# A projection between two large products, in seven half-size products for two row blocks at a time

## The chip, the core and the metric

The kernel runs on one core of a Trainium2 chip. Its engines work side by side, each through its own queue in order: TensorE (PE in the profile; its weight loads are PEld), VectorE (DVE), ScalarE (ACT), GpSimd (POOL) and SyncE (SP), which only issues transfers. Transfers (DMA) are issued from SP's and from POOL's queue. The metric is device time in microseconds, the median of the runs.

## What is computed

Two graph layers on 4096 nodes with 512 features, all in float32. `adj` is 4096 x 4096 and sparse, `W` is 512 x 512.

```python
# layer 0
mask = adj > 0
head = mask / max(sqrt(sum(mask * mask, axis=-1)), EPS)
inc  = adj + head
x = layernorm(x + (inc @ x) / sum(inc, axis=-1))
# layer 1
A2 = adj + eye
dscale = diagonal(A2) ** -0.5
temp = A2 @ x @ W.T
x = layernorm(x + relu((dscale[:, None] * A2 * dscale[None, :]) @ temp))
```

So there are three products with a 4096 x 4096 matrix, and between the second and the third stands the projection by `W.T`, which this change touches.

## The kernel before

All three large products are done by Strassen's scheme in Winograd's form, in which a product of 2 x 2 blocks takes seven block products instead of eight, with sums of blocks before and after. Layer 0 uses one level of it. The products of layer 1 use two: the code numbers them k = 2 (`A2 @ x`) and k = 3 (`A2` times the projected and scaled features).

**Steps of k = 2 and k = 3.** The list `steps` runs over k, over two column halves s, over the seven outer products p in the order of `ORDER[k]`, and over eight blocks kk of the summed dimension. One step (n) is seven matmuls of the inner level, `multiply2`, line 271: 128 x 128 weights are a block of features, the moving operand is 128 x 512 of the adjacency matrix or of sums of its blocks. Each of the seven collects in a PSUM bank of its own (q0 to q6) over the eight kk. The eighth bank, q7, is `spare()`. A float32 matmul shows as two instructions in the profile.

**What VectorE does for a step.** `prepare(n + 2)` (line 226) makes the sums of the adjacency blocks for two steps ahead (`add_up`, lines 166, 168 and 169) in one of three buffers; `sum_b` (lines 255 to 257) makes those of the feature blocks for every second step. In some outer products of k = 2, `prepare` also adds a block of the matrix to a resident one ("raise"), at line 234 before or at line 242 after the sums.

**After eight kk** `outer(k, p, acc)` (line 697) decodes: `inner` (line 676) reads the seven banks and makes four quarters out of them, by two ACT copies into `p1` and `p5` and seven VectorE operations with `u2` and `u3`; each quarter is put straight into a quarter tile of C (`into`) or goes by way of a tile `y` and from there into one or two quarter tiles (`by_way`). For k = 2, p = 7 it goes by way and updates both c21 (line 720) and c22 (line 695) for each of the four parts. Updates of whole quarter tiles, 128 x 2048, are put on the list `deferred`; the loop pops one per step.

**Projection.** C is kept transposed: features on the partitions, nodes along the free dimension. `DONE` says after which p a half of the features' rows is complete: the upper index half h = 1 after p = 7 and h = 0 after p = 3, for each s. Then eight row blocks of 128 nodes go into `queue`, and the loop takes one up per step with 1 <= kk <= 5. `project` (line 748) does four matmuls (line 755) with 512 columns of `wt` into the spare bank; ACT scales the result by `dscale` into a tile z (line 758). For h = 1 the two halves of z are written to DRAM as the operands B21 and B22 of k = 3 (line 760). For h = 0, B11 is written (line 764), B21 and B22 of the same rows are read back (line 763), and one step later `outer_sums` (lines 127 to 133) makes T1 to T4 on VectorE in a tile t, which goes to DRAM (line 769). All these transfers are in POOL's queue. SP loads the operands in `load_b` (line 248), in the order of k = 3: B21, B22, T1, B11, T2, T3, T4.

**Layer 0** shares tiles with it: `combine` (line 494) decodes into two z tiles of four, `layer0` normalises them in place, `operands` (line 533) sends them and their sums t to DRAM.

**The end.** In the last outer product `layer1_first` (line 807) turns back, rectifies and takes statistics of the half of the output features that is already complete. The last three steps are not multiplied in the loop; `finish` (line 826) does their matmuls product by product (line 839), decodes as each comes, turns each of eight row blocks back (`turn`: blocks with r = 0 by two transposes at line 775, blocks with r = 1 by four matmuls that subtract at the same time, lines 863 and 864), rectifies on ACT, adds x on POOL (line 867), takes statistics (`measure`) and normalises and writes out (`leave`), on ACT or VectorE. The order of these calls is written out by hand.

The order of all work is the order of the program text; nothing reorders it. An engine that waits holds up all that stands behind in its queue.

Of the kernel before, what the change touches and what calls it, by code (L numbers as in the profile page):

```python
# [26 lines left out]
def tile_adj_resnorm_d2(  # L27
# [56 lines left out]
    small = ctx.enter_context(tc.tile_pool(name="small", bufs=6))  # L84
# [27 lines left out]
    dscale = const.tile([P, NB], F32, name="dscale")  # L112
    nc.gpsimd.dma_start(out=dscale, in_=diag)
# [80 lines left out]
    queue, later, deferred = [], [], []  # L194
# [31 lines left out]
    def prepare(n):  # L226
# [14 lines left out]
        if k == 2 and p in (1, 2) and kk < EARLY:  # L241
            nc.vector.tensor_add(r, r, a)
# [28 lines left out]
    def multiply2(n, acc, between=None):  # L271
        kk = steps[n][3]
        for m, (right, left) in enumerate(factors(n)):
            if m == 3 and between is not None:
                between()
            nc.tensor.matmul(acc[m], left, right, start=(kk == 0), stop=(kk == NQ - 1))  # L276
# [101 lines left out]
    def spread(j, part):  # L378

        if part == 0:  # L380
            n = small.tile([P, 2], F32, name="n")
# [104 lines left out]
    def take(h, acc):  # L486

        y = row_tile("z", 4)
# [5 lines left out]
    def combine(acc):  # L494

        q1, q2, q6, q5, q7, q3, q4 = acc
        top, low = row_tile("z", 4), row_tile("z", 4)
        p1, p5 = row_tile("p1", 1)[:, 0:W], row_tile("p5", 1)[:, 0:W]
        u2, u3 = row_tile("u2", 1)[:, 0:H], row_tile("u3", 1)[:, 0:H]
        deg = small.tile([P, 2], F32, name="deg")  # L500
# [19 lines left out]
    def layer0(j, C):  # L520

        rd = small.tile([P, 2], F32, name="rd")
# [28 lines left out]
    deg0 = small.tile([P, 2], F32, name="deg")  # L551
# [76 lines left out]
    for n in range(NC, NP * NC):  # L628
# [21 lines left out]
        if j == 1 and c == 1:  # L650
            nc.vector.tensor_scalar(dscale, dscale, 1.0, None, op0=ALU.add)
            nc.scalar.activation(dscale, dscale, AF.Sqrt)
            nc.vector.reciprocal(dscale, dscale)
        if c == 1:
# [15 lines left out]
    wt = accs.tile([P, ND, D], F32, name="wt")  # L670
# [26 lines left out]
    def outer(k, p, acc):  # L697
# [13 lines left out]
        if k == 2:  # L711
# [6 lines left out]
            elif p == 7:  # L718
                def then(i, y):
                    nc.vector.tensor_sub(c21[:, i, :], c21[:, i, :], y)  # L720
                    less(c22[:, i, :], y, c12[:, i, :])
                by_way(then)
# [25 lines left out]
    def project(h, item):  # L748

        j, r, cols = item  # L750
        b = j + h * NP
        pv = spare()
        for f in range(2):
            for e in range(2):
                nc.tensor.matmul(pv, C_of[2][h][f][:, 2 * r + e, cols], wt[:, 2 * f + e, :],  # L755
                                 start=(f + e == 0), stop=(f + e == 2))
        z = row_tile("z", 4)
        nc.scalar.activation(z, pv, AF.Copy, scale=dscale[:, b:b + 1])
        if h:
            nc.gpsimd.dma_start(out=in_outer(3, j, slice(B21, B22 + 1)), in_=split(z))  # L760
            return
        low = split(row_tile("z", 4))
        nc.gpsimd.dma_start(out=low, in_=in_outer(3, j, slice(B21, B22 + 1)))
# [261 lines left out]
```

## Time and profile before

| | before |
|---|---|
| median of the runs | 2298.86 us |
| runs | 2297.68, 2298.86, 3728.19 us |
| profiled execution: time, span | 2299.48 us, 2297.7 us |
| PE busy, share of the span | 2271.1 us, 99% |
| DVE busy | 1797.6 us, 78% |
| ACT busy | 346.8 us, 15% |
| POOL busy | 242.4 us, 11% |
| granted TensorE clock | 0.998 |

"Busy" is time in which an engine executes; the span runs from the first to the last instruction of the profiled execution. "A <- B" in a list of waits means that engine and line A stood idle until B had finished; the numbers are us in total, times, longest. In the order of time each row is the start in us, the duration in us, then engine, line, operation and tiles. The chain that ended last is followed back from the last instruction to what released it.

### The profile page before, as it was taken

Reading aid. Unit: us, or ns where it says so; the run is one execution under the profiler, and the core shown is the slowest. Engines: PE = TensorE matmul, PEld = TensorE weight load, DVE = VectorE, ACT = ScalarE, POOL = GpSimd, SP = SyncE. Lnnn points to the kernel's source line nnn. Section 1 sums busy time; section 2 is a strip of 40 time slices with the busy share of each in tenths; the row PEclk is TensorE's granted clock in tenths of the full one; section 3 lists DMA queues with packets and bytes.
Section 4 is the critical chain, followed back from the end, with each engine's and each line's share of the span. In section 5 each row is a group of like instructions: output and inputs, shape, how many; then the busy total and the mean of one; then the engine's idle time right before and its main releaser. Section 6 shows DMA issues by size and latency. Waiting matters only on the chain.

```text
span 2297.7 us, 20993 instructions
## 1 busy us (share of the span) xinstructions
PE 2271.1 (99%) x7191; PEld 1348.0 (59%) x7191; DVE 1797.6 (78%) x2553; ACT 346.8 (15%) x798; POOL 242.4 (11%) x393
## 2 busy tenths in 40 slices
PE   8999999999999999999999999999999999999997
PEld 6888888888888844444444444444444444444444
DVE  6988898988988787787666778676566788767787
ACT  4333233232231000000000000000000011200013
POOL 0111112211122100000111100010100000100012
PEclk9999999999999999999999999999999999999999
DMA  9788778777876576574566856476665666765672
GB/s 331 268 279 264 261 233 272 273 263 261 249 246 230 203 270 255 190 270 178 231 242 235 296 187 251 158 284 252 236 238 216 226 249 238 256 248 213 225 256 106
DMA packets 149482, 553.64 MB, mean 241 GB/s; under 512 B 16592, under 2 KB 24800, under 8 KB 110976
## 3 DMA queue, kind: packets, MB, share of 16 engines
q1 hardware_dynamic: 114624, 417.38, 51.1%
q0 software_dynamic: 34752, 134.93, 16.5%
q8 instruction: 57, 0.93, 0.2%
q14 instruction: 49, 0.40, 0.1%
HBM read 438.98 MB, written 113.26 MB: 240 GB/s over the span
## 4 chain that ended last, share of the span: by engine, by line
PE 85%; DMA 5%; DVE 4%; issue 4%; ACT 1%; POOL 1%; SPq 0%; ACTq 0%; POOLq 0%; DVEq 0%
PE q L276 55%; PE q L470 25%; PE q L755 5%; DMA nat<-adj 2%; DMA b<-x 1%; DMA a<-adj_r 1%; DVE a L440 1%; DVE mask L433 1%; PE q L775 1%; DVE s L166 1%; ACT nat L330 1%; PE q L839 0%; DVE sr L414 0%; DMA a<-adj_q 0%; DMA oa<-sr 0%
## 5 line engine op out<-in xcount | busy, mean ns | idle before, releaser
L276 PE MATMUL q<-s,ts 128*128 128x512 f32 x1326 | 605.9, 592 | 1.7 <-DVE u L682 1.6
L470 PE MATMUL q<-b,s 128*128 128x256 f32 (+1 forms) x1920 | 454.4, 379 | 0.7 <-DVE s L168 0.7
L276 PEld LDWEIGHTS q<-s,ts 128*128 128x128 f32 x1326 | 251.5, 190 | 318.4 <-issue 289.3
L166 DVE TENSOR_TENSOR s<-a 128x1024 f32<-128x1024 f32 x236 | 288.7, 1223 | 167.7 <-PE q L276 128.9
L470 PEld LDWEIGHTS q<-b,s 128*128 128x128 f32 x1920 | 363.1, 189 | 54.0 <-DVE s L168 1.1
L470 PE MATMUL q<-b,a 128*128 128x258 f32 (+1 forms) x1440 | 352.1, 380 | 1.1 <-ACT p L501 1.1
L276 PE MATMUL q<-a,tr 128*128 128x512 f32 x692 | 325.6, 593 | 1.6 <-DMA a<-adj_r 1.6
L470 PEld LDWEIGHTS q<-b,a 128*128 128x128 f32 x1440 | 272.7, 189 | 40.7 <-ACT p L501 1.5
L276 PE MATMUL q<-s,tr 128*128 128x512 f32 x442 | 225.7, 592 | 0.0
L276 PEld LDWEIGHTS q<-a,tr 128*128 128x128 f32 x692 | 129.3, 190 | 156.0 <-issue 149.2
L330 ACT ACTIVATE nat<-nat,tiny 128x512 f32<-128x512 f32 x240 | 171.3, 717 | 244.0 <-DMA nat<-adj 243.7
L276 PE MATMUL q<-a,ts 128*128 128x512 f32 x346 | 177.0, 593 | 1.2 <-DVE y L687 1.2
L168 DVE TENSOR_TENSOR s<-a,s 128x512 f32<-128x512 f32 x236 | 163.3, 692 | 8.1
L169 DVE TENSOR_TENSOR s<-a,s 128x512 f32<-128x512 f32 x236 | 163.3, 692 | 8.0
L433 DVE SCALAR_TENSOR_TENSOR mask<-a,sc 128x1024 f32<-128x1024 f32 (+2 forms) x129 | 154.1, 1196 | 2.1
L440 DVE TENSOR_TENSOR a<-a,mask 128x1024 f32<-128x1024 f32 x123 | 150.7, 1225 | 6.3
L276 PEld LDWEIGHTS q<-s,tr 128*128 128x128 f32 x442 | 84.0, 190 | 105.7 <-issue 97.6
L680 ACT COPY p<-q 128x512 f32<-128x512 f32 x27 | 15.8, 585 | 730.2 <-PE q L276 730.2
L276 PEld LDWEIGHTS q<-a,ts 128*128 128x128 f32 x346 | 65.5, 190 | 84.9 <-issue 76.1
L755 PE MATMUL q<-wt,c 128*128 128x512 f32 x256 | 115.1, 592 | 0.0
L166 DVE TENSOR_TENSOR s<-r 128x1024 f32<-128x1024 f32 x48 | 58.7, 1223 | 56.2 <-PE q L276 50.8
L276 PE MATMUL q<-r,tr 128*128 128x512 f32 x192 | 90.2, 592 | 0.0
(167 smaller groups left out, 1684.1 us busy)
## 6 DMA issues: line engine op xcount, KB each, us to landing
a<-adj_r SPq DMA_DIRECT2D x112, 1024.0 KB, 6.0
a<-oa SPq DMA_DIRECT2D x80, 1024.0 KB, 5.3
nat<-adj SPq DMA_DIRECT2D x240, 256.0 KB, 7.6
a<-adj_q SPq DMA_DIRECT2D x60, 1024.0 KB, 6.3
tr<-ob SPq DMA_DIRECT2D x112, 512.0 KB, 3.8
oa<-sr POOLq DMA_DIRECT2D x64, 512.0 KB, 7.7
oa<-r POOLq DMA_DIRECT2D x32, 1024.0 KB, 6.1
y<-x POOLq DMA_DIRECT2D x64, 256.0 KB, 6.3
```

The source lines that it names most:

```text
L166: nc.vector.tensor_add(s[:, S3:S1 + 1, :], a[:, A11:A22 + 1, :], a[:, A21, :].unsqueeze(1).to_broadcast([P, 2, w]))
L168: nc.vector.tensor_add(s[:, S2, :], a[:, A11, :], s[:, S1, :])
L169: nc.vector.tensor_add(s[:, S4, :], a[:, A12, :], s[:, S2, :])
L276: nc.tensor.matmul(acc[m], left, right, start=(kk == 0), stop=(kk == NQ - 1))
L330: nc.scalar.activation(y, a, AF.Sign, bias=tiny, scale=2.0 ** 64, accum_out=accum)
L433: nc.vector.scalar_tensor_tensor(m, v, 0.0, s.unsqueeze(1).to_broadcast(list(v.shape)), op0=ALU.is_gt, op1=ALU.mult)
L440: nc.vector.tensor_add(z, z, y)
L470: nc.tensor.matmul(acc[m][:, 0:w], left, b[:, right, 0:w], start=(kk == 0), stop=(kk == NP - 1))
L680: nc.scalar.copy(p1, q1)
L755: nc.tensor.matmul(pv, C_of[2][h][f][:, 2 * r + e, cols], wt[:, 2 * f + e, :], start=(f + e == 0), stop=(f + e == 2))
L775: nc.tensor.transpose(ps[:, at + i * P:at + (i + 1) * P], C_of[3][h][d // 2][:, 2 * r + d % 2, cols], ident)
```

## The change

Two row blocks, r = 0 and r = 1 of the same n, are projected together as a 2 x 2 block product: their C blocks (r by feature half f) times `wt` (feature half f by output half). `wt` holds seven operands, four loaded and T1 to T4 computed once in step 4 (T4 is then taken as one of the seven). The seven products are of two matmuls with 256 columns each into the spare bank, ACT copies each out into one of eight half tiles, and they stand between the matmuls of three successive steps. The four sums of C blocks are made on Pool, the combinations of the products on DVE. The eight blocks of a half become four pairs; two of them are begun per outer product, at kk = 2 and kk = 4.

T2, T3 and T4 of k = 3 are no longer made from a read-back: the half h = 1 writes its share (with a negative scale `nscale` where it is needed), and the half h = 0 adds its own to it in DRAM by accumulating DMAs.

Around it: the decode of p = 7 goes straight into c22, and both updates are deferred; the raises of line 242 are held until after the decode; while pairs are waiting, all deferred updates are done at once. z tiles are two instead of four, some pools of small tiles shrink. In the last outer product the addition of x in `layer1_first` moves from DVE to Pool and ahead by a step. In `finish` the last quarter is decoded, subtracted on DVE and turned back ahead of the remaining statistics, all eight blocks by transposes, and which blocks ACT normalises is set by hand.

```diff
-    small = ctx.enter_context(tc.tile_pool(name="small", bufs=6))
+    small = ctx.enter_context(tc.tile_pool(name="small", bufs=4))
@@ prepare
-            nc.vector.tensor_add(r, r, a)
+            raises.append(lambda: nc.vector.tensor_add(r, r, a))
@@ multiply2
-            if m == 3 and between is not None:
-                between()
+            if m in between:
+                between[m]()
@@ combine
-        top, low = row_tile("z", 4), row_tile("z", 4)
+        top, low = row_tile("z", 2), row_tile("z", 2)
@@ outer, k == 2
             elif p == 7:
-                def then(i, y):
-                    nc.vector.tensor_sub(c21[:, i, :], c21[:, i, :], y)
-                    less(c22[:, i, :], y, c12[:, i, :])
-                by_way(then)
+                into(c22)
+                deferred.extend((lambda: nc.vector.tensor_sub(c21, c21, c22), lambda: less(c22, c22, c12)))
@@ project
-        pv = spare()
-        for f in range(2):
-            for e in range(2):
-                nc.tensor.matmul(pv, C_of[2][h][f][:, 2 * r + e, cols], wt[:, 2 * f + e, :],
-                                 start=(f + e == 0), stop=(f + e == 2))
-        z = row_tile("z", 4)
-        nc.scalar.activation(z, pv, AF.Copy, scale=dscale[:, b:b + 1])
...
+    def project(h, s, n, first):
+        cols = slice(n * P, (n + 1) * P)
+        a11, a12, a21, a22 = (C_of[2][h][f][:, 2 * r:2 * r + 2, cols] for r in range(2) for f in range(2))
+        if first:
+            pools["places"] = [t[:, i * H:(i + 1) * H] for t in (row_tile(t, 1) for t in ("p1", "p5", "u2", "u3")) for i in range(2)]
+        places = [pools["places"][i] for i in (range(7) if first else (7, 1, 0, 6, 3, 2, 4))]
+        q = []
+        def product(left, right):
+            def now():
+                ps = spare()[:, 0:H]
+                for e in range(2):
+                    nc.tensor.matmul(ps, left[:, e, :], wt[:, right, e, :], start=(e == 0), stop=(e == 1))
+                q.append(places[len(q)])
+                nc.scalar.copy(q[-1], ps)
+            return now
+        def sums():
+            s1, s2, s3, s4 = (y[:, 2 * i:2 * i + 2, :] for y in (row_tile("y", 2, (P, 4, P)) for _ in range(2)) for i in range(2))
+            nc.gpsimd.tensor_add(s1, a21, a22)
+            nc.gpsimd.tensor_add(s2, a11, s1)
+            nc.gpsimd.tensor_add(s3, a11, a21)
+            nc.gpsimd.tensor_add(s4, a12, s2)
+            return s1, s2, s3, s4
+        if first:
+            yield {1: product(a11, B11), 3: product(a12, B21), 5: product(a22, T4)}
+            s1, s2, s3, s4 = sums()
+            yield
+            yield {1: product(s2, T2), 3: product(s3, T3), 5: product(s1, T1)}
+            yield
+            yield {1: product(s4, B22)}
+        else:
+            yield {4: product(a11, B11)}
+            s1, s2, s3, s4 = sums()
+            yield
+            yield {1: product(a12, B21), 3: product(a22, T4), 5: product(s2, T2)}
+            yield
+            yield {1: product(s3, T3), 3: product(s1, T1), 5: product(s4, B22)}
+        q1, q2, q4, q6, q7, q5, q3 = q
+        z = [row_tile("z", 2) for _ in range(2)]
+        nc.vector.tensor_add(z[0][:, 0:H], q2, q1)
+        nc.vector.tensor_add(q6, q6, q1)
+        nc.vector.tensor_add(q7, q7, q6)
+        nc.vector.tensor_add(q6, q6, q5)
+        nc.vector.tensor_add(z[0][:, H:D], q3, q6)
+        nc.vector.tensor_sub(z[1][:, 0:H], q4, q7)
+        nc.vector.scalar_tensor_tensor(z[1][:, H:D], q7, -1.0, q5, op0=ALU.mult, op1=ALU.subtract)
+        t = row_tile("t", 1, (P, 4, H))
+        for r in range(2):
+            nc.vector.tensor_sub(t[:, 2 * r, :], z[r][:, 0:H], z[r][:, H:D])
+        for r in range(2):
+            leave_operands(h, r * NQ + s * SB + n, z[r], t[:, 2 * r, :], t[:, 2 * r + 1, :])
+        yield
+    def leave_operands(h, j, z, t, m):
+        b = j + h * NP
+        def scaled(o, y, by=dscale):
+            nc.scalar.activation(o, y, AF.Copy, scale=by[:, b:b + 1])
+        def put(op, y, **how):
+            nc.gpsimd.dma_start(out=in_outer(3, j, slice(op, op + 1)), in_=y.unsqueeze(1), **how)
+        first, second = z[:, 0:H], z[:, H:D]
         if h:
+            scaled(m, second, nscale)
+            scaled(z, z)
+            scaled(t, t)
             nc.gpsimd.dma_start(out=in_outer(3, j, slice(B21, B22 + 1)), in_=split(z))
+            put(T2, m)
+            put(T3, second)
+            put(T4, t)
+        else:
+            scaled(m, t, nscale)
+            scaled(t, t)
+            scaled(first, first)
+            scaled(second, second, nscale)
+            put(B11, first)
+            put(T1, t)
+            put(T2, m, accum_op=ALU.add)
+            put(T3, second, accum_op=ALU.add)
+            put(T4, m, accum_op=ALU.add)
@@ layer1_first
+            nc.gpsimd.tensor_add(o[:, H:D], o[:, H:D], y[:, H:D])
...
-                add(o[:, H:D], y[:, H:D])
@@ finish
-            if i < 2:
-                nc.vector.tensor_sub(c21[:, i, :], y, c21[:, i, :])
-            else:
-                lower[i] = y
+            nc.vector.tensor_sub(c21[:, i, :], y, c21[:, i, :])
...
         measure(0)
         measure(1)
-        leave(0)
+        put(2, lambda o: nc.vector.tensor_sub(o, acc[q4], u3))
+        for t in range(4, 8):
+            turn(t)
         measure(2)
-        leave(1)
-        put(2, lambda o: nc.vector.tensor_sub(o, acc[q4], u3))
-        turn(4)
         measure(3)
-        leave(2)
-        turn(5)
-        leave(3)
+        leave(0, True)
+        leave(1, False)
+        leave(2, True)
         measure(4)
...
@@ the loop
-        if deferred:
+        while deferred:
             deferred.pop(0)()
+            if not pairs:
+                break
+        between = {3: lambda: take_up(items.pop(0))} if len(items) > 1 else {}
+        if kk in (2, 4) and pairs:
+            going.append(project(*pairs.pop(0), kk == 2))
+        for pair in going:
+            between.update(next(pair))
         if n < len(steps) - TAIL:
-            multiply2(n, acc, (lambda: take_up(items.pop(0))) if len(items) > 1 else None)
+            multiply2(n, acc, between)
...
+        elif n == 4:
+            outer_sums(wt[:, T1:T4 + 1], wt[:, B11], wt[:, T4], wt[:, B21], wt[:, B22])
...
+        for pair in going[::-1]:
+            next(pair)
+        if kk in (4, 6):
+            del going[:1]
...
+        while raises:
+            raises.pop(0)()
```

## The prediction

> **What bounds the kernel now.** I read four views in this order: the page's busy table, the chain that ended last, the list of what TensorE (PE) waited for, and the order of time at two places.
>
> ```profile
> PE 2271.1 (99%) x7191; PEld 1348.0 (59%) x7191; DVE 1797.6 (78%) x2553; ACT 346.8 (15%) x798; POOL 242.4 (11%) x393
> PE 85%; DMA 5%; DVE 4%; issue 4%; ACT 1%; POOL 1%; SPq 0%; ACTq 0%; POOLq 0%; DVEq 0%
> ...
> 124.75 533.41 PE q L470 x2460
> ...
> 1061.08 3.43 PE q L755 x8
> 1064.51 6.01 PE q L276 x14
> ```
> PE is busy throughout and 85% of the chain is PE, so a removed matmul is worth its full time if nothing new makes PE wait. The last three rows give prices. One step (14 instructions of 512 columns) is 6.01 us, 0.429 each. The projection of one row block (8 such) is 3.43 us. In layer 0, 2460 instructions of some 256 columns take 533.41 us, 0.217 each: half the columns cost half the time.
>
> ```profile
> PE q L863 <- DVE y L911: 2.9, 1, 2.9
> PE q L276 <- DVE u L682: 1.6, 2, 0.8
> ...
> PE q L276 <- DVE y L687: 1.2, 2, 0.6
> ...
> PE q L839 <- DVE s L168: 0.7, 1, 0.7
> ```
> These are PE's waits outside layer 0's start that the change touches (us in total, times, longest). L682 and L687 are the decode of outer product 7 in the first chain of products, twice; L839 and L863 are the tail.
>
> **Projection: PE.** It goes: 32 blocks of 3.43 us, 109.8 us. It gets 16 pairs of 7 products, each 2 matmuls of 2 instructions with 256 columns: 28 x 0.217 = 6.07 us a pair, 97.1 us. **-12.6 us**, all on the chain. The interleaving costs PE nothing by itself: the transposes (L775) in the last outer product lie between matmuls and the steps around them keep 6.01.
>
> **Decode of product 7.** The order of time at the first of the two places:
>
> ```profile
> 1044.76 2.29 DVE r L242
> 1047.04 0.61 DVE y L681
> 1047.65 0.02 issue
> 1047.68 0.69 DVE c L720
> 1048.37 0.60 DVE c L695
> 1048.97 0.61 DVE u L682
> ```
> Each PSUM read is followed by two updates of C (L720, L695), and ahead of it all VectorE (DVE) does the 2.29 us raise of L242. PE's step begun at 1046.92 takes until 1054.90, 7.98 us instead of 6.01: 1.97 lost; the second place (1440.32 to 1448.45) lost 2.12. The change decodes straight into C, which is one operation per read as for products 4, 5 and 1 (no PE wait there), does the updates (2.29 + 2.28) in the next step, and moves all raises behind the decode. **-4.0 us.** The raises issue no DMA; what they hold longer is the slot of their `a` tile, so SP's next load into it may start later, but PE reads that tile later than the raise. What is late next: DVE now has 2.6 (operand sums) + 1.5 (feature sums) + 4.6 + 2.3 = 11 us in that step of 6.01. Counting on from the decode, the second prepare behind it ends about 18.6 us after the step's start and PE needs it at 20.6: 2 us to spare, because the step ahead of it is longer by three products.
>
> **Projection: DVE, ACT and Pool.** Per pair DVE gets 9 operations of 128x256 at the spacing of L127/L132 (0.34, dependent 0.45): 3.3 us; gone are four per block in one half (64 x about 0.36 = 23 us), added 53: 30 us net over the some 490 us of these stages, in which DVE was busy 323. ACT gets 7 PSUM copies (0.37, L489) and 6 or 8 scalings a pair; a 128x256 one out of SBUF is not in the trace: 0.37 (L779's spacing) to 0.82 (L161, twice the width), I take 0.48 (L161's spacing of 0.70 less 256 columns of L779). Pool gets four adds a pair (L867, 0.72) and 8 or 10 DMA issues, 0.54 to 0.91 each where the rows show them: 8 to 10 us a pair, with a pair every some 16 us. All this is covered if it keeps up, and there are three new waits to check.
> First, PE waits at each product for the ACT copy of the one before (one PSUM bank): two matmuls lie between, 1.72 us, against about 0.6. But ACT is in order, and the first pair's scalings, which wait for DVE, stand ahead of the second pair's copies. Counted from the start of the step in which the first pair ends (7.75 us long: 6.01 and two products): DVE's prepare starts at -0.66 (its buffer is free before the step's last matmul) and takes 2.58, sum_b 1.50, so the combination starts at 3.4, its differences t end at 6.5 and 6.8; ACT is through at 9.5 (upper half) to 10.5 (lower half), the blocked copy at 10.9 at the latest, and PE needs it at 11.2. It holds with 0.3 to 1.3 us; a DVE 1.5 us late costs PE a microsecond, and so does ACT at 0.82.
> Second, the combination of the second pair waits in DVE's queue for its last product, one matmul before its step's end; the next prepare starts 1.7 us late, and the decode after it still frees each bank 1.2 us or more before PE returns to it.
> Third, z and t are reused 16 us later: two z tiles instead of four, so DVE waits there for five DMAs a block, among them the accumulating ones, which the trace does not show. Their issue is bounded by 0.54 and 0.91, their landing by 2.0 and 10.2 us (least and most of the ob writes). Even 10.2 fits, the last being issued about 13 us into the cycle and t needed at 24. SP's loads of T1 to T4 come at least a product later. In layer 0 the second pair of z goes too: combine at 608.44 would write the tiles that operands sent off at 589.49, landed by 600. Tile pools of 4 or 2 for statistics are still behind their last reader. I take nothing for all three but a margin: **+3 us** for first pairs (8 x about 0.4).
>
> **Pool against DVE.** L867 takes 0.719 us at least, 0.724 in the median and 1.227 at most, in the row of four that begins beside DVE's two-input L904; L842, 128x128, took 1.05 beside L168, which kept its 0.69. So Pool gave way there; DVE's L886 took 0.88 instead of 0.55 under Pool.
> The Trainium skill, "SBUF — State Buffer", section "Who interferes with whom", speaks against the change: a DVE instruction with two SBUF inputs and a GpSimd one that reads SBUF hold one port pair in turn, the first for its whole length. By the rows DVE loses up to 0.33 us per add and Pool most; by the page DVE may lose a whole add each time, and the sum of this prediction would have up to 50 us less in hand on DVE. The trace has no add under a stream of two-input DVE operations.
>
> **wt.** Four loads instead of one (3 x 0.75 us of Pool) and four sums of 512 (2.8 us of DVE) in step 4, where DVE is catching up after 838 and the decode at 852.22 has 2.4 us in hand: **+0.5 us**.
>
> **Tail.**
>
> ```profile
> 2268.63 3.70 PE L839 MATMUL q<-s,ts 128*128 128x512 f32 x8 [0.71 <-DVE s L168]
> ...
> 2282.95 0.69 DVE L911 TENSOR_TENSOR y<-q,u 128x512 f32<-128x512 f32 x1
> ...
> 2283.78 0.77 PE L863 MATMUL q<-ident,y 128*128 128x128 f32 x2 [2.86 <-DVE y L911]
> ...
> 2290.93 0.72 POOL L867 TENSOR_TENSOR o<-o,y 128x256 f32<-128x256 f32 x1 [1.36 <-ACT o L779]
> ```
> Four adds (4 x 0.35) leave DVE ahead of the last prepare: the stall of 0.9 us at 2268.6 goes, if Pool has them done. The product q4 is ready at about 2281.0, but L911 queues behind measure and leave until 2282.95. Moved ahead, with two more subtractions (2 x 0.69, one of them before), the transposes start at about 2282.5 instead of 2283.8 and are 4 per block instead of 8. Pool's last add starts near 2286.1 instead of 2290.9. Then ACT and DVE are late: seven normalisations, four measures and the roots, moved behind the four rectifies, run to about 2292.1 where they ended at 2294.2. **-2.1, with the stall -3.0 us.**
>
> **Sum.** -12.6 - 4.0 - 3.0 + 3.0 + 0.5 = -16.1. The profiled execution took 2299.48 (span 2297.7 and 1.8 around it), the median of the runs shown is 2298.86: 2299.48 - 16.1 = 2283.4, less 0.6: **2283**.
>
> **Rivals.**
> A, *the small waits eat it* (0.20): ACT's scalings cost 0.82, or DVE comes late, and each of the 16 pairs stalls PE by about 0.8 us more: 2283 + 13 = 2296, 2291 to 2304. For: the margin of 0.3. Against: DVE stands idle 1 to 5 us before most prepares there.
> B, *Pool's sums hold up DVE* (0.13), slower than before: every add costs DVE its whole 0.79 us (L867's mean), 3.1 a pair, and it surfaces in PE: 50 us less what is in hand; with the gain of 19 the sum is +31, 2330. Place: the step in which the first pair is combined. It decides from the point where DVE is over 1.5 us late there; break-even with before at 1.2 us a pair. Against: Pool gave way in the rows.
> C, *accumulating DMAs occupy Pool* (0.04): if one issue took 5 us, six a pair would make Pool, which also does the next sums, slower than the cycle of 16 us: 8 pairs x 15 = 120, 2400. No row speaks for it.
> D, *the smaller products are not cheaper*: 28 x 0.245 would equal two blocks; it would give 2296 with the other gains. Layer 0's rate excludes nearly all of it; it is in A's chance.
>
> **Numbers.** Forecast 0.62 (2276 to 2291: with no stalls at all, wt hidden and the tail at its best 2278), A 0.20, B 0.13, C 0.04, a gain over 2% 0.01. Range 2274 to 2306, forecast and A. A measurement here tells 2%, 46 us, from no change: faster 0.01; same 0.95; slower 0.04 (C and the far end of B).
>
> **What would show it.** PE's busy time some 16 us lower with the new products at 0.217 an instruction; waits on L682 and L687 gone; few waits of PE on ACT copies; ACT done before PE returns; the last Pool add within 6 us of the last transpose. Wrong would make it: PE waiting for DVE's prepare or for an ACT copy in the steps with pairs (A, B), long gaps between Pool's DMA issues (C).

## The result and the profile after

| | before | after |
|---|---|---|
| median of the runs, side by side | 2298.27 us | 2283.56 us |
| ratio | | 0.9941, interval 0.9928 to 0.9955 |
| profiled execution: time, span | 2299.48, 2297.7 us | 2284.03, 2282.1 us |
| layer 0, up to the first step of k = 2 | 804.41 us | 803.35 us |
| from there to the first matmul of `finish` | 1456.47 us | 1445.97 us |
| from there to the end | 36.82 us | 32.78 us |

The medians differ by 14.7 us, 0.6%, which is no change by the bound of 2% but well resolved. One execution of the kernel before, 3728.19 us, was a slow one; the ratio goes by the fast ones alone and makes it 13.6 us. In the lines after, the code stands two lines lower than before up to `prepare`, and elsewhere at new places: the steps' matmuls are L278, a product L766, its ACT copy L768, the sums on Pool L773 to L776, the combination L795 to L804, the scalings L816, the transfers L819 and L826, the matmuls of `finish` L908.

The last three rows of the table are the quickest way to split the difference: -1.1 in layer 0, which the change hardly touches, -10.5 in the long products with the projection, -4.0 at the end. The page after, with the busy table and the engines' shares of the chain that ended last:

```profile
PE 2255.1 (99%) x7359; PEld 1380.3 (60%) x7359; DVE 1854.4 (81%) x2619; ACT 417.3 (18%) x991; POOL 383.3 (17%) x548
...
PE 89%; DVE 5%; DMA 3%; ACT 2%; issue 1%; POOL 0%; SPq 0%; DVEq 0%; ACTq 0%
```

PE's busy time fell by 16.0 us with 168 instructions more. DVE's rose by 56.8 us, where 30 were forecast; that is the first sign that something beside the new operations happened to DVE. The list of PE's waits after:

```profile
...
PE q L766 <- ACT p L768: 4.3, 8, 0.9
PE q L844 <- DVE c L913: 1.8, 1, 1.8
PE q L278 <- DMA a<-adj_r: 1.8, 1, 1.8
```

The waits for the decode of product 7 (lines 682 and 687 before) are gone, and so are those of the tail, apart from one of 1.8 us. New is one kind: eight waits, one per first pair, of a product for the ACT copy of the product before it. The wait for adjacency (`adj_r`) was there before, at 1.6 us; it comes near 835 us, ahead of the projection.

**What a product costs.** The mean durations of matmuls overlap one another, since these are pipelined; the chain that ended last gives the pace (start, us, what). One product:

```profile
1059.24 0.86 PE q L766 x4
```

Four instructions take 0.86 us, 0.215 each, so a pair takes 28 x 0.215 = 6.02 us and 16 pairs 96.3 us, where the 32 blocks took 109.8: -13.5.

**The decode of product 7**, in order of time:

```profile
1046.21 1.88 PE L278 MATMUL q<-a,tr 128*128 128x512 f32 x4
...
1047.49 0.68 DVE L692 SCALAR_TENSOR_TENSOR c<-u,p 128x512 f32<-128x512 f32 x1
...
1052.22 1.88 PE L278 MATMUL q<-a,tr 128*128 128x512 f32 x4
```

The step lasts from 1046.21 to 1052.22, 6.01 us, where it was 7.98. The last read of PSUM begins at 1047.49; the raise (from 1048.09) and the two updates (from 1054.40 and 1056.72, 2.29 us each) stand behind it.

**The end**: the transposes of the last four blocks and Pool's last four additions:

```profile
2270.24 1.06 PE L844 MATMUL q<-ident,c 128*128 128x128 f32 x8 [1.85 <-DVE c L913]
...
2271.23 2.95 POOL L922 TENSOR_TENSOR o<-o,y 128x256 f32<-128x256 f32 x4 [1.76 <-ACT o L848]
```

Pool is done 2.9 us after the last transpose. The last normalisation, on DVE, ends at 2278.3 of a span of 2282.1; before it was 2294.2 of 2297.7.

**The new wait.** The third and last step of a first pair, in which the second pair begins, in order of time. PE's step begins at 1075.42; the second pair's product with a22 comes in the step after, at 1087.05:

```profile
1074.76 1.47 DVE L167 TENSOR_TENSOR s<-a 128x1024 f32<-128x1024 f32 x1 [0.20 <-PE q L278]
...
1075.23 1.59 POOL L774 TENSOR_TENSOR y<-c,y 128x256 f32<-128x256 f32 x1
1075.42 1.02 PE L278 MATMUL q<-a,tr 128*128 128x512 f32 x2
1076.27 1.10 DVE L169 TENSOR_TENSOR s<-a,s 128x512 f32<-128x512 f32 x1
...
1077.40 1.26 DVE L170 TENSOR_TENSOR s<-a,s 128x512 f32<-128x512 f32 x1
...
1078.59 1.21 DVE L257 TENSOR_TENSOR ts<-tr 128x512 f32<-128x512 f32 x1
...
1080.63 0.42 DVE L795 TENSOR_TENSOR z<-p 128x256 f32<-128x256 f32 x1
...
1086.25 0.49 ACT L816 ACTIVATE t<-t,dscale 128x256 f32<-128x256 f32 x1
...
1086.65 0.35 ACT L768 COPY p<-q 128x256 f32<-128x256 f32 x1
...
1087.05 1.13 PE L766 MATMUL q<-wt,c 128*128 128x256 f32 x4 [0.29 <-ACT p L768]
```

Read it downwards. While Pool makes the block sums of the second pair, DVE's additions with two inputs take 1.47 (L167, from 1074.76), 1.10, 1.26 and 1.21 us instead of 1.22, 0.69, 0.69 and 0.68: 1.76 us lost. The combination of the first pair (L795) begins 5.2 us after the step's start, not 3.4. ACT scales what the combination makes, and its last scaling ends at 1086.74. The copy of the second pair's product out of the one spare bank stands behind that and ends at 1087.00; PE stands for 0.29 us and its restart costs some 0.3 more. In the lower half, with eight scalings instead of six, it is 0.7 to 0.9 us.

### The profile page after: what moved, and what is told of

It reads as the page before. It is cut to its first block, busy times and chain, and to the rows that moved or that the text cites. A ratio compares the mean times of both kernels' runs of the same rounds, so it can differ in the third digit from the quotient of the medians.

```text
span 2282.1 us, 22004 instructions
## 1 busy us (share of the span) xinstructions
PE 2255.1 (99%) x7359; PEld 1380.3 (60%) x7359; DVE 1854.4 (81%) x2619; ACT 417.3 (18%) x991; POOL 383.3 (17%) x548
## 4 chain that ended last, share of the span: by engine, by line
PE 89%; DVE 5%; DMA 3%; ACT 2%; issue 1%; POOL 0%; SPq 0%; DVEq 0%; ACTq 0%
PE q L278 55%; PE q L472 27%; PE q L766 3%; PE q L485 2%; DMA nat<-adj 2%; DVE s L167 1%; PE q L908 1%; PE q L844 1%; DVE s L169 0%; ACT z L816 0%; ACT nat L332 0%; DVE a L442 0%; DVE mask L435 0%; ACT t L816 0%; DVE ts L257 0%
## 5 line engine op out<-in xcount | busy, mean ns | idle before, releaser
L278 PE MATMUL q<-s,ts 128*128 128x512 f32 x1326 | 612.2, 592 | 0.1
L472 PE MATMUL q<-b,s 128*128 128x256 f32 (+1 forms) x1920 | 454.4, 379 | 0.0
L278 PEld LDWEIGHTS q<-s,ts 128*128 128x128 f32 x1326 | 251.6, 190 | 299.1 <-issue 268.3
L167 DVE TENSOR_TENSOR s<-a 128x1024 f32<-128x1024 f32 x236 | 290.2, 1230 | 161.4 <-PE q L278 131.3
L472 PEld LDWEIGHTS q<-b,s 128*128 128x128 f32 x1920 | 363.1, 189 | 53.1 <-DVE z L510 0.5
L472 PE MATMUL q<-b,a 128*128 128x258 f32 (+1 forms) x1440 | 352.5, 380 | 0.7 <-ACT p L503 0.6
L278 PE MATMUL q<-a,tr 128*128 128x512 f32 x692 | 329.4, 592 | 1.8 <-DMA a<-adj_r 1.8
L472 PEld LDWEIGHTS q<-b,a 128*128 128x128 f32 x1440 | 272.5, 189 | 40.9 <-ACT p L503 1.5
L278 PE MATMUL q<-s,tr 128*128 128x512 f32 x442 | 225.7, 592 | 0.0
L278 PEld LDWEIGHTS q<-a,tr 128*128 128x128 f32 x692 | 129.5, 190 | 145.1 <-issue 138.9
L278 PE MATMUL q<-a,ts 128*128 128x512 f32 x346 | 176.8, 592 | 0.0
L169 DVE TENSOR_TENSOR s<-a,s 128x512 f32<-128x512 f32 x236 | 167.7, 711 | 8.1
L170 DVE TENSOR_TENSOR s<-a,s 128x512 f32<-128x512 f32 x236 | 167.3, 709 | 8.0
L278 PEld LDWEIGHTS q<-s,tr 128*128 128x128 f32 x442 | 84.0, 190 | 92.1 <-issue 84.6
L684 ACT COPY p<-q 128x512 f32<-128x512 f32 x27 | 15.6, 577 | 631.5 <-PE q L278 631.5
L278 PEld LDWEIGHTS q<-a,ts 128*128 128x128 f32 x346 | 65.7, 190 | 83.0 <-issue 76.1
L425 POOL DMA_DIRECT2D oa<-sr x64 | 57.7, 902 | 283.8 <-DVE sr L416 181.6
L873 POOL DMA_DIRECT2D out<-o x24 | 13.1, 547 | 507.8 <-ACT o L162 507.8
L278 PE MATMUL q<-r,tr 128*128 128x512 f32 x192 | 92.7, 593 | 0.0
```

The costliest lines, as they stand in the source:

```text
L167: nc.vector.tensor_add(s[:, S3:S1 + 1, :], a[:, A11:A22 + 1, :], a[:, A21, :].unsqueeze(1).to_broadcast([P, 2, w]))
L169: nc.vector.tensor_add(s[:, S2, :], a[:, A11, :], s[:, S1, :])
L170: nc.vector.tensor_add(s[:, S4, :], a[:, A12, :], s[:, S2, :])
L425: nc.gpsimd.dma_start(out=dst, in_=sr.rearrange("p m (k i) -> p (m k) i", i=P))
L472: nc.tensor.matmul(acc[m][:, 0:w], left, b[:, right, 0:w], start=(kk == 0), stop=(kk == NP - 1))
```

## The experiments

Four questions: where do the 6.5 us of stalls with restarts come from (the eight gaps in PE's order of time are 0.46, 0.48, 0.91, 0.90, 0.45, 0.48, 1.03, 0.91, each with some 0.1 behind it), what are the decode and the end worth alone, do the accumulating transfers cost anything, and can the stalls be had back. "Region" below is the second stretch of the first table, from the first step of k = 2 to `finish`, 1445.97 us for the changed kernel. It holds the wait for adjacency near 835, which the edits don't aim at and which differs from one profiled execution to the next: nothing in the list of run 3, 0.6 us in run 12, 1.8 in the changed kernel's first profile, 2.6 in run 10. So two regions can differ by some 2 us for that alone. All medians are over at least five runs beside runs of the kernel before on the same chip.

### 1. Products one matmul later

```diff
-            yield {1: product(a12, B21), 3: product(a22, T4), 5: product(s2, T2)}
+            yield {2: product(a12, B21), 4: product(a22, T4), 6: product(s2, T2)}
```

> The three products of the second pair in step kk = 5 stand one matmul later (before the third, fifth and seventh matmul instead of the second, fourth and sixth); nothing else. Theory: PE waits once per first pair, 0.45 to 0.48 us for the upper half and 0.90 to 1.03 for the lower (plus 0.11 for starting again, 6.5 us over eight pairs), because the ACT copy of the step's first product stands behind the scalings of the first pair; a product that comes 0.86 us later waits for 0 and about 0.1. The waits of PE's products on ACT copies go from 4.3 to under 0.8 us, the span from 2282.1 to about 2276, the time from 2283.6 to about 2277.5. Rival: the wait is for something that moves with the product (a copy that is slow by itself, the restart of PE); then the waits stay and the time is 2283.6.

2282.89 us, ratio 0.9945 (0.9932 to 0.9957), region 1445.48: nothing gained. The wait on L768 is gone from the list, but two others have come in its place:

```profile
PE q L278 <- ACT p L684: 1.8, 2, 1.4
...
PE q L278 <- DVE c L685: 0.5, 1, 0.5
```

Both are the decode, in the lower half alone. The chain of work leads back from the first of them:

```profile
1210.58 11.93 DMA ob<-t
...
1222.66 0.36 DVE t L804
...
1226.69 0.48 ACT p L684
```

A transfer out of t lands 11.9 us after its issue. T1 and the accumulated T2 and T4 all leave from there; by the order of the issues this one, the last of its pair, is the accumulated T4. The second pair's differences (L804), which write that t, wait for it; its eight scalings come late on ACT, the decode's copy (L684) stands behind them, and PE's next step waits for the bank. This was the prediction's third wait, for which it took nothing of its own.

The second place, near 1290, cost more than its waits: 1.44 us on L684 and 0.46 us on L685, 1.1 us apart, and then the granted clock was 0.50 from 1291.08 to 1294.49, which made PE 1.8 us later. By the gaps in PE's order of time the decode took 4.9 of the 6.5 us, slow clock and restarts included.

### 2. No block sums

```diff
-            s1, s2, s3, s4 = (y[:, 2 * i:2 * i + 2, :] for y in (row_tile("y", 2, (P, 4, P)) for _ in range(2)) for i in range(2))
-            nc.gpsimd.tensor_add(s1, a21, a22)
-            nc.gpsimd.tensor_add(s2, a11, s1)
-            nc.gpsimd.tensor_add(s3, a11, a21)
-            nc.gpsimd.tensor_add(s4, a12, s2)
-            return s1, s2, s3, s4
+            return a21, a11, a21, a12
```

> Left out: the four sums of C blocks on Pool; the products read single C blocks in their place, so the projected values are not the reference's. PE, ACT, DVE and all transfers have the same instructions. Theory: Pool's adds (1.1 to 1.6 us each instead of 0.72) and DVE's two-input operations hold each other up; without them L169 and L170 are back from 1.10 to 0.69 us in the steps with pairs, the combination of the first pair starts 1.7 us earlier, ACT is through before PE returns, and PE's waits on the copies vanish: 2283.6 - 6.5 = 2277. Rival: ACT's scalings are too long by themselves or DVE is late for another reason; the waits stay at about 0.3 and 0.8 us, 2283.6.

2276.76 us, ratio 0.9915 (0.9900 to 0.9929), region 1438.77, 7.2 us less, of which 0.7 is the wait for adjacency. None of the eight waits on the copies is left. The same place without Pool beside it:

```profile
1076.77 0.69 DVE L169 TENSOR_TENSOR s<-a,s 128x512 f32<-128x512 f32 x1
...
1079.63 0.42 DVE L790 TENSOR_TENSOR z<-p 128x256 f32<-128x256 f32 x1
```

The step began at 1076.17 (0.86 before the product at 1077.03); the combination starts 3.5 us later, as forecast, and the copy ends at 10.0, 1.2 ahead of PE. DVE's busy time is 1827.2 us, 29.6 above the kernel before: the forecast 30 for the new operations alone. The other 27.2 us of the changed kernel are lengthening under Pool: 0.43 us in the mean for each of 64 additions.

### 3. The decode as it was

```diff
-            raises.append(lambda: nc.vector.tensor_add(r, r, a))
+            nc.vector.tensor_add(r, r, a)
@@ p == 7
-                into(c22)
-                deferred.extend((lambda: nc.vector.tensor_sub(c21, c21, c22), lambda: less(c22, c22, c12)))
+                def then(i, y):
+                    nc.vector.tensor_sub(c21[:, i, :], c21[:, i, :], y)
+                    less(c22[:, i, :], y, c12[:, i, :])
+                by_way(then)
```

> The decode of product 7 by way of y with its two updates per part, and the raises ahead of the decode, as in the kernel before; all else as changed. Theory: the stall of 1.97 and 2.12 us of PE at the two places comes back: 2283.6 + 4.1 = 2287.7, with the waits on the second VectorE operation of the decode again at about 0.8 us twice. Rival: the load that DVE waited for ahead of the first place was the cause, and it is gone for another reason; then 2283.6.

2287.87 us, ratio 0.9966 (0.9953 to 0.9980), region 1448.52. The median is as expected, its make-up is not:

```profile
PE q L278 <- DVE ts L258: 2.5, 2, 1.3
...
PE q L278 <- DVE y L691: 0.8, 2, 0.6
```

The decode's own waits are 1.3 us (0.5 of it on L686) instead of the 2.8 us in the list of before. The rest moved: DVE, late from the decode and now under the first pair's block sums too, makes the feature sums (L258) too late for PE. What the old decode costs shows at another place in this kernel, but it is again near 4 us: 4.3 by the medians, 3.3 against run 12; in the profiles the region is only 2.6 us longer, but it lacks the changed kernel's wait for adjacency, 1.8 us. The run takes the decode and the raises back together, so how the 4 us divide between the two stays open.

### 4. The end as it was

`finish` is as before the change: two of the four feature blocks of the last quarter are subtracted on PE again (`lower`, `minus`), the last quarter is decoded behind the first normalisations, and x is added on DVE for the first half.

```diff
-        put(2, lambda o: nc.vector.tensor_sub(o, acc[q4], u3))
-        for t in range(4, 8):
-            turn(t)
+        leave(0)
         measure(2)
...
+        put(2, lambda o: nc.vector.tensor_sub(o, acc[q4], u3))
+        turn(4)
```

> The end as before: the order written out in finish, the subtraction by matmuls for the blocks with r = 1, and the addition of x in layer1_first on DVE a step later. Theory: the stretch from the first matmul of finish to the end goes from 32.8 back to 36.8 us, PE's wait for the last operand sums (0.7 us) and the wait for the last quarter (2.9 us) are back: 2283.6 + 4.0 = 2287.6. Rival: the gain at the end came with the earlier finish of other work (loads of x in time); then less than 2 us comes back.

2288.13 us, ratio 0.9965 (0.9952 to 0.9979). The stretch from `finish` to the end is 35.48 us, 2.70 more than in the changed kernel, and the two waits of before are there again, 0.7 us on L169 and this one:

```profile
PE q L932 <- DVE y L980: 2.9, 1, 2.9
```

Yet before the change this stretch was 36.82 us, 1.34 longer, with the same waits. The windows of the two show why. First the kernel before, behind its wait of 2.86 us (the columns are the window, its length, busy time and instructions of PE, PEld, DVE, ACT and POOL, then the granted clock, the DMA share and GB/s), then the run with the old end:

```profile
2283.70:2286.50 2.80, 2.72 (x13) 2.75 (x14) 1.05 (x4) 0.63 (x2) 0.08 (x1) 0.50 0.49 187
```

```profile
2274.90:2277.00 2.10, 2.02 (x18) 2.05 (x19) 1.22 (x5) 0.66 (x2) 0.30 (x1) 1.00 0.39 144
```

After a wait of the same length the clock was 0.50 in the one execution and 1.00 in the other, and the transposes ran at half their pace for 2.8 us. So of the 4.04 us at the end 2.7 are the change and 1.3 a slow restart that went with the wait. The medians lie further apart than 2.7, by 4.6 us, or 3.6 against run 12. Between the two profiled executions, 5.3 us apart, 3.0 us stand in layer 0, where this one has a wait of 2.1 us on L393, which the edit doesn't touch.

### 5. The block sums on DVE, in the same place

```diff
-            nc.gpsimd.tensor_add(s1, a21, a22)
+            nc.vector.tensor_add(s1, a21, a22)
```

and the same for s2, s3 and s4.

> The four block sums are made by DVE instead of Pool, at the same place of the order, so ahead of the combination of the first pair on DVE's queue. Theory (the stretched DVE instructions beside Pool's sums make the first pair late): DVE's additions of 128x512 are back at 0.69 us, as in the run without sums, but four additions of about 0.42 us each, 1.7 us, now stand ahead of the combination. It starts at about 3.4 + 1.7 = 5.1 us after the step's start, where the changed kernel had 5.2, so the stalls on the copies of the products stay: 2283.5, plus or minus 1.5. Rival (the additions are only stretched, and what is late is late for another reason, the scalings on ACT or the transfers): the same work on DVE costs 1.7 us a pair where DVE is waited for, 16 x 1.7 = 27 us at most, and half of that is seen: 2290 to 2297.

2294.66 us, ratio 0.9989 (0.9979 to 0.9998), region 1456.80, 10.8 us more than the changed kernel; some 2 us of that are the wait for adjacency, 2.5 here, with a clock of 0.50 behind it from 837.18 to 840.59. The number is the rival's, its reason is not; the waits show two things:

```profile
...
PE q L766 <- DVE y L774: 6.4, 2, 3.2
PE q L766 <- ACT p L768: 3.5, 4, 0.9
```

The theory's stalls on the copies do stay, in the lower half. But the larger cost comes at only two places, the first pair of each s, where neither theory had looked: there the sums stand on DVE's queue behind the raises and the sums of two steps, and the product that reads s2 waits 3.2 us. Behind that wait PE runs slowly, by the window (columns as in run 4):

```profile
1073.20:1077.00 3.80, 3.70 (x8) 2.38 (x9) 3.15 (x5) 0.37 (x1) 0.00 (x0) 0.62 0.06 24
```

The granted clock is 0.62 in these 3.8 us: 0.50 from 1072.70 to 1076.11, so for 3.4 us, and 1.00 after that. The two waits cost 4.8 and 4.9 us in all, by the gaps in PE's order of time.

The Trainium skill, "TensorE: Matmul & The Clock Gate", section "Part 1: The HAM clock gate (the "warmup" mystery)", gives about 3.4 us of idleness as what halves the clock, and about as long a busy time to get it back. The runs here agree on the time to get it back: each slow stretch behind such a wait lasts 3.4 us, one in run 10 twice that. They show the slow clock after waits of 2.9 and 3.2 us already, after 2.9 us in some executions and not in others, and in run 1 after 1.44 and 0.46 us.

### 6. The block sums on DVE, behind the older pair's combination

```diff
-        for pair in going[::-1]:
+        for pair in going:
```

together with the edit of run 5.

> As the run before it, but of two pairs that share a step the older one goes first, so the four sums on DVE stand behind the combination of the first pair. Theory: the combination starts at 3.4 us after the step's start as forecast, the scalings are through by 9.5 to 10.5, and the waits for the copies of the products, 6.5 us with their restarts, go as they went in the run without sums: 2277, and the output is whole. Rival: the sums come 4 to 5 us later than the products that read them allow, and a wait of the product on the sums takes the place of the one on the copies: 8 waits of 0.5 to 1 us, 2281 to 2285.

2289.13 us, ratio 0.9964 (0.9951 to 0.9977), region 1448.94. All eight waits on the copies are gone, as the theory said; the two waits of 3.2 us at the first pair of each s remain, 10.2 us with their restarts and the slow clock. Taking these off gives 1438.7. Both numbers of the expectation, 2277 and 2281 to 2285, are missed by these two places: the rival had such waits, but at all eight first pairs and of at most 1 us.

### 7. Plain transfers

```diff
-            put(T2, m, accum_op=ALU.add)
-            put(T3, second, accum_op=ALU.add)
-            put(T4, m, accum_op=ALU.add)
+            put(T2, m)
+            put(T3, second)
+            put(T4, m)
```

> The three accumulating DMAs of a lower pair become plain ones, so that T2 to T4 of the lower half hold only the last term. Theory: no engine waits for their landing in the changed kernel, and their issue takes Pool time that nothing waits for, so the time stays: 2283.5, plus or minus 1. Rival (accumulating transfers occupy Pool and so delay the block sums, or load the DMA queues that the operands come by): 8 lower pairs of which each gains 0.5 to 2.5 us: 2263 to 2280.

2284.46 us, ratio 0.9946 (0.9931 to 0.9961), region 1445.08. The changed kernel loses nothing by accumulating. The price is there all the same, on Pool. The transfers out of t on L819, by the view of that line (durations in ns: min, median, max; first and last start in us), first in the changed kernel, then here:

```profile
L819 POOL DMA_DIRECT2D ob<-t x80: 540/742/2639, 1085.8 to 1679.3; - x80
...
DMA to landing us min/median/max: 2.0/3.6/12.9
```

```profile
L819 POOL DMA_DIRECT2D ob<-t x80: 540/540/560, 1085.8 to 1679.2; - x80
...
DMA to landing us min/median/max: 2.0/2.4/8.8
```

Spans on Pool are rough, but the plain form is 0.54 to 0.56 us each time and the accumulating one up to five times that. The landings are those of all transfers on L819.

### 8. Products one matmul later, with plain transfers

The edits of runs 1 and 7.

> The later products of the first run together with plain transfers, so T2 to T4 of the lower half hold only the last term. Theory (with the later products, the buffers z and t of the lower half's second pair wait for accumulating transfers that land 12 us after they start, and the decode comes late by it): the plain ones land in 2.6 to 3.0 us, the stalls at 1227 and 1289 to 1296 go, 5.4 us: 2277.5, plus or minus 1. Rival (the stalls come from the order of ACT's copies, which the later products moved): as with the later products alone, 2282.9.

2279.24 us, ratio 0.9922 (0.9908 to 0.9936), region 1440.18, 5.3 less than run 1. The waits on L684 and L685 and the slow clock behind them are gone with the accumulation, so run 1's explanation stands: most of the gain of the later products was eaten by the landing of the accumulating transfers. The expected 2277.5 is missed by 1.7 us; in the profiled execution layer 0 took 807.27 us, 3.9 more than in the changed kernel.

### 9. Sums divided between Pool and DVE

```diff
+            by = nc.gpsimd if first else nc.vector
-            nc.gpsimd.tensor_add(s1, a21, a22)
+            by.tensor_add(s1, a21, a22)
...
-        for pair in going[::-1]:
+        for pair in going:
```

> The first pair's block sums stay on Pool; the second pair's go to DVE, behind the combination of the first pair. The output is whole. Theory (the 6.5 us are lost where the second pair's sums on Pool stretch DVE's additions ahead of the first pair's combination, and the run with all sums on DVE lost its gain only at the first pair of each s, where PE waited 3.2 us twice for sums that stood behind the raises and the sums of the bands on DVE): both kinds of stall are gone, DVE has 8 x 1.7 = 14 us more to do in which nothing waits for it, and the time is that of the run without sums: 2277, plus or minus 1.5. Rival (any sums on Pool stretch what the first pair's combination waits for, the first pair's own sums too): half the stalls stay, 2280 or later. Second rival (14 us more on DVE make the second pair's combination, and behind it the decode, late): new waits of PE on the copies or the decode, 2282 or later.

2278.12 us, ratio 0.9924 (0.9911 to 0.9938), region 1438.40, 7.6 less than the changed kernel, of which 1.1 is the wait for adjacency and 6.5 are the eight waits with their restarts. In order of time, at the same place (PE's step begins at 1075.10):

```profile
1078.55 0.42 DVE L796 TENSOR_TENSOR z<-p 128x256 f32<-128x256 f32 x1
...
1084.75 0.37 ACT L768 COPY p<-q 128x256 f32<-128x256 f32 x1
...
1086.27 1.03 PE L766 MATMUL q<-wt,c 128*128 128x256 f32 x4
```

The combination starts 3.45 us after the step (forecast 3.4), ACT is through with the scalings at 9.5 (forecast 9.5), the copy at 10.0, and PE comes at 11.2 without a wait. The second pair's sums begin on DVE at 1082.15 and take 0.42 us apiece, against means of 1.0 to 1.5 on Pool in the changed kernel.

### 10 and 11. All but one pair of each s on DVE

Run 10 has `nc.gpsimd if h == 0 and n == 0 else nc.vector`, and that is not what its expectation describes: the half h = 1 is projected first, so the two pairs left on Pool were the first of the lower half, and the first pair of each s was on DVE. Run 11 has `h == 1 and n == 0`.

> As the run beside it, but only the first pair of each s, two of the 16, has its sums on Pool; the other 14 have theirs on DVE, behind the combination of an older pair where there is one. The output is whole. Theory: no sums on Pool lie beside a combination in either, so this one too is at 2277, plus or minus 1.5; of the two stalls of 3.2 us and their restarts at a slower clock nothing is left. Rival (the sums of the other first pairs come late on DVE as well, since the raises and band sums stand ahead of them): PE waits for the sums at some of the six other first pairs, 0.5 to 3 us each: 2280 to 2290. If Pool beside DVE costs DVE anything that PE sees outside the combinations, this one is faster than the run beside it by that much.

> What the run on a single pair of each s should have been: the upper half is projected first, so its first pair (h = 1, n = 0), not that of the lower half, has its sums on Pool now; the other 14 pairs have theirs on DVE behind the older pair's combination. The output is whole. Theory (the stall of 3.2 us comes only where the sums on DVE stand in the step in which the raises and the deferred updates are caught up with, that is at the first pair of an s): both stalls and their restarts are gone, 9 to 12 us less than with the wrong pair: 2277 to 2279. Rival (the stall belongs to any first pair that follows on decoding, so it shows at the lower half's first pair as well when that one is on DVE): two stalls of 3.2 us and restarts remain, 2286 to 2290.

Run 10: 2288.94 us, ratio 0.9970 (0.9958 to 0.9981), region 1451.70. As the edit stands it is run 6 with another pair on Pool, and it has the same two waits of 3.2 us. Run 11: 2277.35 us, ratio 0.9917 (0.9903 to 0.9930), region 1438.64, and of PE's waits only one is left inside the region, 1.0 us for adjacency near 835; the other four of its list are layer 0 (L343, L472 twice) and the end (L845). The lower half's first pair makes its sums on DVE without a wait, so the rival of run 11 falls: it is the caught-up work at the start of an s that made DVE late.

### 12. The changed kernel again, beside run 11

> The changed kernel as it is, on the same chip and beside the same runs of the kernel before as the run ahead of it, so that the two can be compared directly. Theory: 2283.5, plus or minus 1, with the eight waits on the copies of the products, and 5 to 7 us above the run with the sums divided between DVE and Pool. Rival (the differences of 5 us between runs on different chips are differences between chips): the two agree within 2 us.

2284.55 us, ratio 0.9950 (0.9936 to 0.9964), region 1444.72, with the eight waits on L768 and 4.3 us again. On the same chip run 11 is 7.2 us faster, and the two intervals don't touch. So run 11 beats both kernels. Run 9, on another chip, is without the eight waits too and its region is within 0.3 us of run 11's, though its interval overlaps that of the changed kernel a little; between runs 9 and 11 nothing can be told.

## Why the prediction was right, point by point

The forecast of 2283.0 met 2283.56, and the range held it. In part the terms made up for one another:

| step | forecast | measured | from |
|---|---|---|---|
| projection on PE | -12.6 | -13.5 | 0.215 an instruction in the chain, not 0.217 |
| decode of product 7 | -4.0 | -4.1 | step 6.01 instead of 7.98, and the second place alike |
| waits of the first pairs | +3.0 | +6.5 | eight gaps with their restarts |
| `wt` | +0.5 | +0.1 | gaps near 852 |
| the end | -3.0 | -4.0 | 36.82 to 32.78 |
| layer 0 | 0 | -1.1 | 804.41 to 803.35 |
| adjacency late at 835 | 0 | +0.3 | 1.73 to 1.99 us |
| not assigned | 0 | +0.3 | |
| sum | -16.1 | -15.5 | 2299.48 to 2284.03 |

**Projection: right.** Half the columns cost half the time. Rival D fell with it. No run puts the old projection back alone; the 13.5 us stand on the pace of the products in the chain and on PE's busy time, 16.0 us less.

**Decode: right**, with its reason: one operation per PSUM read, the rest behind. The 4.6 us of updates and the raise cost PE nothing where they now stand, as the 2 us to spare had said.

**Waits of the first pairs: right mechanism, wrong size.** The step that failed is that the combination "starts at 3.4". Without Pool's sums it does (runs 2, 9); under them it starts at 5.2. The prediction read from one place of the tail that Pool gives way, and allowed DVE 0.33 us per addition at most. Under a stream of DVE instructions both lose: 0.43 us per Pool addition for DVE in the mean (1.76 us in the four instructions shown), and Pool's additions took medians of 1.1 and 1.6 us on L773 and L774 instead of 0.72. The page of the Trainium skill that was weighed there, "SBUF — State Buffer", section "Who interferes with whom", had the direction right, that DVE loses too. The prediction's reading of it was a whole addition, 0.79; the rows' bound was 0.33, and 0.43 lies between, nearer to the rows. The price was not what was missing: the count that ends at 3.4 holds no loss of DVE at all, though four additions at 0.33 make 1.3 us, as much as the largest margin that it found. The prediction's sentence that DVE 1.5 us late costs PE a microsecond was close: 1.8 us late cost 0.4 to 1.0. Of the signs that it named, PE's busy time, the decode's waits and Pool's last addition came as it said; "ACT done before PE returns" did not, and PE's waits for an ACT copy were its sign of being wrong. That the number came so close is luck: the 3.5 us that these waits cost over the 3.0 set aside were nearly made up by four other terms, 2.4 us better than forecast together, and by layer 0.

**Rivals A and B** were this mechanism at a higher price. ACT's scaling was 0.49 to 0.51 us, where 0.48 was taken and 0.82 was A's condition. B's break-even was 1.2 us a pair; it was 0.4, the 6.5 us over 16 pairs. B also named the place rightly: the step in which the first pair is combined. **Rival C** fell with run 7; accumulating transfers cost Pool at most 2.6 us per issue, not 5, and PE sees none of it. But "even 10.2 fits" held by its slack, not by its number: landings reached 12.9 us in the changed kernel, and in run 1, where the order left less room, they cost most of what the later products had gained.

**The end: right, with 1.3 us of luck** in the execution it was read from: 2.7 by run 4, the rest a half clock after the wait that was removed.

**What stays open.** The 1.1 us of layer 0 lies within what other runs show there (802.8 to 807.3 us), and the 0.3 us at 835 within the spread of that wait, so neither is an effect of the change that can be shown. The smaller pools and the two z tiles were not tried alone.

## What to carry to other kernels

Work given to an idle engine isn't free if it lengthens what the busy engine does beside it: ask which of those instructions is waited for, and leave the work with the busy engine, behind its urgent part, where that costs less. A stall removed by shifting the order shows the next one at once (here the landing of transfers whose tile is reused), so see what the freed time runs into before counting the gain.

## What the runs showed of the hardware

- Pool's additions of 128x256 that read SBUF and DVE's with two SBUF inputs lengthened one another: DVE's 128x512 from 0.69 to 1.10 and 1.26 us, Pool's from 0.72 to 1.17 and 1.59. Sixty-four such additions made DVE 27.2 us busier and took 82 us of Pool instead of the 46 that 64 x 0.72 would be.
- The transfers of 128 KB on L819 landed in 2.0, 3.6 and 12.9 us (min, median, max) and took Pool up to 2.6 us to issue while those of T2 to T4 in the lower half accumulated; with plain ones it was 2.0, 2.4 and 8.8 us, and 0.56 at most. It stays unseen while the tile isn't wanted again.
- After PE had waited 2.86 us (before, at the end) and 3.2 us (six places in runs 5, 6 and 10) the granted clock was 0.50 for 3.4 us, at one place of run 10 for 6.8; the waits of 3.2 us cost 4.8 to 5.1 us in all, that one 6.3. After 2.85 us in run 4 and 2.6 us in run 10 (near 835) it stayed 1.00, while in run 1 waits of 1.44 and 0.46 us close together were followed by 0.50 for 3.4 us. So the length of one wait alone does not decide it.
